# Source order on VectorE and GpSimd ahead of the queries, and one scaling for two input norms

## The chip, the cores and the metric

The kernel runs on one core of one Trainium2 chip. The metric is the device time of one execution in microseconds (us), lower is better. The time of the kernel before is the median of three runs.

## The reference, cut to what matters

A layer of cross attention with a position bias and a mask, then a gated feed-forward layer. Everything is float32: 8 batches of 128 tokens, 512 features, 32 heads of 128, 1376 inner features.

```python
x = x + xattn(layernorm(x), ctx, mask, bias, ...)   # EPS = 1e-5
x = x + ffn(layernorm(x), ...)

def xattn(hidden, kv, ...):
    h = hidden * rsqrt(mean(hidden**2) + EPS) * ln_weight
    q, k, v = h @ w_q.T, kv @ w_k.T, kv @ w_v.T     # 32 heads
    p = softmax(where(mask, q @ k.T + bias, -inf))
    return hidden + (p @ v) @ w_out.T
```

So the attention's input is normalised twice: a layer norm takes away the mean and divides by sqrt(v + EPS), v being the variance; then an RMS norm divides by the root mean square of the result, and multiplies by `ln_weight`. The mean square after the first norm is v / (v + EPS). Both divisions together are one: by sqrt(v (1 + EPS) + EPS²).

## The kernel before

**Stages.** The heads are worked in 8 groups of 4. A prologue loads the context (already transposed), the weights of the first keys and values and the inputs, computes the keys and values of group 0, and normalises and transposes the inputs of the 8 batches. Then come the query projections of all 8 groups, which are stored to DRAM; then attention, group by group, with the keys and values of the next group computed in between; the output projection; the second norm and the feed-forward layer. The diff touches only what is issued ahead of the queries.

**Projections with seven products.** Each projection is a 2x2 block product by Strassen's scheme as Winograd orders it: seven products of half-size blocks in place of eight. GpSimd makes four sums of weight blocks (`sums_a`, lines L194 to L197: s1, s2, a block replaced in place, s4), in a tile `S_k`, `S_v` or `S_q`. Four sums of token blocks (`sums_b`, L202 t1, L203 t2, L204 `b12` replaced in place, L205 t4) are made once for the context (`ctx_sb`) and once for the normed inputs (`hT`); three run on VectorE, L204 on GpSimd.

`seven` then issues the products in the order 2, 1, 6, 7, 4, 5, 3, each for two tiles, and yields after each tile. Products 2, 6, 7 and 4 end with a ScalarE copy out of the PSUM bank (L236, L246). Products 1, 5 and 3 end with a VectorE add (L241 for product 1, L252 for 5 and 3). Products 1, 6, 7 and 4 build up in the same two PSUM banks, so product 6 of a tile can't start before product 1's add has read it, and product 7 not before product 6's copy. Product 6 uses the weight sum s2 and the token sum t2, product 7 the replaced blocks, product 4 the token sum t4.

Of the 28 yields of the prologue (n = 0 to 27), the first 4 are the products 2 and 1 of the keys, then 4 of the values, 10 more of the keys, 10 more of the values. A matmul in float32 shows up as two instructions in the profile, so one product of the keys with its two tiles is eight of them.

**Norms.** For each batch, `norm1` takes the moments (`bn_stats`, `bn_aggr`), the root of the variance (`rstd_of`: a VectorE step, a ScalarE square root, a VectorE reciprocal), subtracts and scales on VectorE into y (L167), squares y on ScalarE with a sum (L172), makes a second root from it, and scales y into `hn` on ScalarE (L176). `norm1_T` transposes `hn` on TensorE (L153), and VectorE multiplies the transposed block by `ln_weight` into `hT` (L181). Before, `norm1` of batch b is called at n = 5 + 2b and `norm1_T` at n = 11 + 2b.

**What sets the order.** Each engine runs its own queue in order. The order within a queue is chosen by the framework's planner: it simulates the program with a cost model and takes, for each engine, the instruction that comes first in the source among those that are ready in the simulation. Source order is thus a priority and not the order. Buffers of a pool (three y slots of tag "s", which the attention's bias additions of L297 use later; four `hn`; two S tiles; three weight tiles) are handed on when their readers are done. Loads are issued on the SP queue (the first weights on ScalarE's).

Of the kernel before, what the change touches and what calls it, by code (L numbers as in the profile page):

```python
# [10 lines left out]
F32 = mybir.dt.float32  # L11
U8 = mybir.dt.uint8
AF = mybir.ActivationFunctionType
ALU = mybir.AluOpType
# [3 lines left out]
P = 128  # L18
BS = 32
EPS = 1e-5  # L20
MASKED = 3.0e38
FLOOR = -1.0e38
TINY = 1.0e-30


@with_exitstack
def xattn_ffn_kernel(
# [19 lines left out]
    nc = tc.nc  # L47
    B, S, D = x.shape
# [13 lines left out]
    ADD, SUB = ALU.add, ALU.subtract  # L62
# [11 lines left out]
    work = pool("work", 2, side="right", reuse_waits="tile")  # L74
    small = pool("small", 4, side="right", reuse_waits="tile")
# [22 lines left out]
    ctx_sb = toks.tile([P, DC + 3, T], F32, tag="ctx", name="ctx_sb")  # L98
# [22 lines left out]
    x_in = [acts.tile([P, 2, D], F32, tag="a", name=f"x_{i}") for i in range(B // 2)]  # L121
    for b in range(B):
        nc.sync.dma_start(x_in[b // 2][:, b % 2, :], x[b])
    q_w = {0: load_q(0)}

    lnw_sb = const.tile([P, DC], F32, name="lnw_sb")
    nc.gpsimd.dma_start(lnw_sb, lnw.rearrange("(c p) -> p c", p=P))
    mask_u8 = work.tile([P, B, S], U8, tag="tt", name="mask_u8")
# [12 lines left out]
    def rstd_of(dst, src, scale):  # L141

        nc.vector.tensor_scalar(dst, src, scale, EPS, ALU.mult, ALU.add)
        nc.scalar.activation(dst, dst, AF.Sqrt)
        nc.vector.reciprocal(dst, dst)

    def moments(mv, b, st, src):
        nc.vector.bn_stats(st, src)
        nc.vector.bn_aggr(mv[:, b, :], st)
# [6 lines left out]
    hT = hpool.tile([P, DC + 3, T], F32, tag="hT", name="hT")  # L156
    mv1 = const.tile([P, B, 2], F32, name="mv1")
    rs1 = const.tile([P, B], F32, name="rs1")

    def norm1(b):  # L160
        st = small.tile([P, nc.vector.BN_STATS_DIM], F32, tag="st", name=f"st_{b}")
        xb = x_in[b // 2][:, b % 2, :]
        moments(mv1, b, st, xb)
        rs = rs1[:, b : b + 1]
        rstd_of(rs, mv1[:, b, 1:2], 1.0)
        y = work.tile([P, D], F32, tag="s", name=f"y_{b}", bufs=3)
        nc.vector.tensor_scalar(  # L167
            y, xb, mv1[:, b, 0:1], rs, ALU.subtract, ALU.mult
        )
        sq = work.tile([P, D], F32, tag="aT", name=f"sq_{b}")  # L170
        ss = small.tile([P, 1], F32, tag="ss", name=f"ss_{b}")
        nc.scalar.activation(sq, y, AF.Square, accum_out=ss)  # L172
        rr = small.tile([P, 1], F32, tag="rr", name=f"rr_{b}")
        rstd_of(rr, ss, 1.0 / D)
        hn = work.tile([P, D], F32, tag="pT", name=f"hn_{b}", bufs=4)
        nc.scalar.activation(hn, y, AF.Copy, scale=rr)  # L176
        return b, hn

    def norm1_T(b, hn):
        tp = transposed(hn, ps_tp.tile([P, DC, P], F32, tag="pt", name="tp"))  # L180
        nc.vector.tensor_tensor(  # L181
            hT[:, :DC, bass.ts(b, S)], tp, lnw_sb.unsqueeze(2).to_broadcast([P, DC, P]), ALU.mult
        )

# [7 lines left out]
    def sums_a(eng, a11, a12, a21, a22, s1, s2, s4):  # L192

        eng.tensor_tensor(s1, a21, a22, ADD)  # L194
        eng.tensor_tensor(s2, s1, a11, SUB)
        eng.tensor_tensor(a21, a11, a21, SUB)
        eng.tensor_tensor(s4, a12, s2, SUB)  # L197
        return {1: a11, 2: a12, 3: s4, 4: a22, 5: s1, 6: s2, 7: a21}

    def sums_b(eng, b11, b12, b21, b22, t1, t2, t4, eng3=None):  # L200

        eng.tensor_tensor(t1, b12, b11, SUB)  # L202
        eng.tensor_tensor(t2, b22, t1, SUB)  # L203
        (eng3 or eng).tensor_tensor(b12, b22, b12, SUB)  # L204
        eng.tensor_tensor(t4, b21, t2, SUB)  # L205
        return {1: b11, 2: b21, 3: b22, 4: t4, 5: t1, 6: t2, 7: b12}

    def combine_rows(name, w):

        a11, a12 = w[:, :HC, :HW], w[:, HC:, :HW]  # L210
        a21, a22 = w[:, :HC, HW:], w[:, HC:, HW:]
        s = spool.tile([P, 3, HC, HW], F32, tag="S", name=f"S_{name}")
        s1, s2, s4 = s[:, 0], s[:, 1], s[:, 2]
        return sums_a(nc.gpsimd, a11, a12, a21, a22, s1, s2, s4)

    def combine_tokens(src):

        b11, b12 = src[:, :HC, :512], src[:, :HC, 512:]
        b21, b22 = src[:, HC:DC, :512], src[:, HC:DC, 512:]
        t1, t2, t4 = (  # L220
            src[:, DC + i, :].rearrange("p (c n) -> p c n", c=HC) for i in range(3)
        )
        return sums_b(nc.vector, b11, b12, b21, b22, t1, t2, t4, nc.gpsimd)

    def seven(name, tiles, product, part, pool, tag="mm"):


        def bank(i):
            return [
                pool.tile([P, 512], F32, tag=tag, name=f"mm_{name}_{i}_{t}") for t in tiles  # L230
            ]

        m = bank(2)
        for t in tiles:
            product(2, t, m[t], True)
            nc.scalar.copy(part(1, 1, t), m[t])  # L236
            yield
        m = bank(1)
        for t in tiles:
            product(1, t, m[t], True)  # L240
            nc.vector.tensor_tensor(part(1, 1, t), part(1, 1, t), m[t], ADD)  # L241
            yield
        for i, r, c in ((6, 1, 2), (7, 2, 2), (4, 2, 1)):
            for t in tiles:
                product(i, t, m[t], False)
                nc.scalar.copy(part(r, c, t), m[t])  # L246
                yield
        m = bank(5)
        for i, r, c in ((5, 2, 2), (3, 1, 2)):
            for t in tiles:  # L250
                product(i, t, m[t], i == 5)
                nc.vector.tensor_tensor(part(r, c, t), part(r, c, t), m[t], ADD)  # L252
                yield

    def project_T(name, w, src, heads):

        for j in range(GH):
            heads.append(acts.tile([P, T], F32, tag="a", name=f"{name}_{j}"))

        def product(i, t, out, first):  # L260
            for c in range(HC):
                nc.tensor.matmul(  # L262
                    out, w[i][:, c, bass.ts(t, P)], src[i][:, c, :],
                    start=(first and c == 0), stop=(c == HC - 1), skip_group_check=True,
                )

        def part(r, c, t):
            return heads[2 * (r - 1) + t][:, bass.ts(c - 1, 512)]

        yield from seven(name, range(2), product, part, ps_mm)  # L270
# [22 lines left out]
    def probabilities(g, b, qT, kT, pb):  # L293
# [22 lines left out]
        ri = small.tile([P, GH], F32, tag="ri", name=f"ri_{n}")  # L316
        nc.vector.tensor_scalar_max(ri, sm, TINY)
        nc.vector.reciprocal(ri, ri)
# [53 lines left out]
    def kv(g, out):  # L372
        wk, wv = kv_w.pop(g)
        kT, v = [], []
        out[g] = kT, v
        keys = project_T(f"k{g}", combine_rows(f"k{g}", wk), ctx_t, kT)
        if g:
            yield from keys
            yield from project_V(f"v{g}", combine_rows(f"v{g}", wv), ctx_t, v, ps_mm)
        else:  # L380

            yield from itertools.islice(keys, 4)
            values = project_V(f"v{g}", combine_rows(f"v{g}", wv), ctx_t, v, ps, "sc")
            yield from itertools.islice(values, 4)
            yield from keys
            yield from values


    queries = [dram.tile([P, GH, T], F32, name=f"queries_{g}") for g in range(NG)]
    ctx_t = combine_tokens(ctx_sb)  # L390
    kvs = {}
    normed = []
    for n, _ in enumerate(kv(0, kvs)):
        if n % 2 == 1 and 5 <= n < 5 + 2 * B:
            normed.append(norm1((n - 5) // 2))
        if n % 2 == 1 and 11 <= n < 11 + 2 * B:
            norm1_T(*normed.pop(0))
    for n in normed:
        norm1_T(*n)
    h_t = combine_tokens(hT)  # L400

    res_scale = const.tile([P, B], F32, name="res_scale")
    res_bias = const.tile([P, B], F32, name="res_bias")
    nc.vector.tensor_scalar_add(res_scale, rs1, 1.0)
    nc.vector.tensor_tensor(res_bias, mv1[:, :, 0], rs1, ALU.mult)
    nc.vector.tensor_scalar_mul(res_bias, res_bias, -1.0)
# [85 lines left out]
    for g in range(NG):  # L492
        kT, v = kvs.pop(g)
# [89 lines left out]
    for i in range(B // 2):  # L583
# [8 lines left out]
        m = by_product(banks)  # L592
        x1.append(acts.tile([P, 2, D], F32, tag="a", name=f"x1_{i}"))
        for k in range(2):
            b = 2 * i + k
# [3 lines left out]
                bias=res_bias[:, b : b + 1], scale=res_scale[:, b : b + 1],  # L599
# [63 lines left out]
    for y in ys:  # L663
        norm2_T(*y)
    t1, t2, t3, t4 = (
        acts.tile([P, HC, 512], F32, tag="a", name=f"T{n}_h2") for n in range(1, 5)
    )
# [7 lines left out]
    for i in range(NP):  # L675
        ws, gate = [], [acts.tile([P, T], F32, tag="a", name=f"gate_{i}_{r}") for r in range(2)]
        for nm, w in zip("gu", gate_up[i]):
            s = fw.tile([P, 3, HC, P], F32, tag="S", name=f"S_{nm}{i}")
# [16 lines left out]
        def part(r, c, t):  # L695
            return (gate[r - 1], act[2 * i + r - 1])[t][:, bass.ts(c - 1, 512)]
# [16 lines left out]
    for b in range(B):  # L713
        r = work.tile([P, D], F32, tag="aT", name=f"r_{b}")
        parts = 1 if b + 1 < B else 2
        for k in range(parts):
            cols = bass.ts(k, D // parts)
            o = ps.tile([P, D // parts], F32, tag="m", name=f"dn_{b}_{k}")
            for n, ic in enumerate([NI - 1, *range(NI - 1)]):
                m = min(P, INTER - ic * P)  # L720
# [50 lines left out]
```

## Time and profile before

| | us |
|---|---|
| median of 3 runs | 1152.23 (1151.07 to 1153.02) |
| the profiled execution, its own time | 1152.01 |
| its span in the profile | 1150.2 |
| TensorE busy (matmul) | 1120.0, 97% of the span |
| VectorE busy | 502.3, 44% |
| ScalarE busy | 318.1, 28% |
| GpSimd busy | 297.9, 26% |
| start of the first query product | 68.9 |

Engines in the profile: PE is TensorE's matmul, PEld its weight load, DVE VectorE, ACT ScalarE, POOL GpSimd, SP the queue of SyncE that issues DMAs. A group's row gives line, engine, operation, out<-in, number, busy time and mean ns. A timeline row gives start and duration in us from the start of the span; the brackets tell how long the engine was idle before it and what released it. A windows row gives a stretch, busy time with the number of instructions for each engine, the granted TensorE clock (1.00 is full), the DMA share, and GB/s.

### The profile page before, as it was taken

What the parts mean: (1) busy time and instruction counts of PE and PEld (TensorE: products, weight loads), DVE (VectorE), ACT (ScalarE), POOL (GpSimd) and SP (SyncE); (2) the same over time, 40 slices, a digit from 0 to 9 for tenths busy, and PEclk for the clock granted to TensorE, in tenths of its full rate; (3) what the DMA queues carried; (4) which work ended last, traced back from release to release, by engine and by line L of the source; (5) the groups of instructions that cost most, each with busy time, mean ns of one, the idle gap of its engine ahead of it and who ended that gap; (6) DMA issues with size and microseconds to landing.
All of it is one profiled execution on the core that took longest, in us unless ns stands there. A gap on an engine that the chain in (4) does not pass through costs nothing.

```text
span 1150.2 us, 12321 instructions
## 1 busy us (share of the span) xinstructions
PE 1120.0 (97%) x4286; PEld 731.4 (64%) x4286; DVE 502.3 (44%) x957; ACT 318.1 (28%) x899; POOL 297.9 (26%) x255
## 2 busy tenths in 40 slices
PE   6999999999999999999999999789999999999998
PEld 3564444445867777686958689678888864444445
DVE  4541111116555555555555557824433242434311
ACT  2521112223444344444344443301000022223000
POOL 5331221116333333333223315620000034220000
PEclk9999999999999999999999999899999999999999
DMA  9114432257555455555554347865232332110000
GB/s 284 41 37 149 175 114 110 110 197 259 175 166 175 151 186 174 168 182 183 179 173 152 129 139 218 275 192 171 78 104 65 109 128 73 36 37 1 18 29 28
DMA packets 117533, 154.38 MB, mean 134 GB/s; under 512 B 12032, under 2 KB 71680, under 8 KB 117472
## 3 DMA queue, kind: packets, MB, share of 16 engines
q1 hardware_dynamic: 114784, 149.93, 40.3%
q10 hardware_dynamic: 2192, 2.10, 0.6%
q0 software_dynamic: 496, 1.58, 0.4%
q8 instruction: 34, 0.56, 0.2%
q14 instruction: 27, 0.22, 0.1%
HBM read 101.14 MB, written 52.43 MB: 134 GB/s over the span
## 4 chain that ended last, share of the span: by engine, by line
PE 91%; DVE 4%; DMA 2%; ACT 1%; issue 1%; POOL 0%; SPq 0%; ACTq 0%; DVEq 0%
PE mm_q L262 17%; PE mm_v L280 16%; PE m L470 16%; PE mm_k L262 16%; PE mm_f L690 9%; PE dn L721 7%; PE sc L302 4%; PE av L358 4%; DMA wk<-in_wkT_dram 1%; DMA wo<-in_woT_dram 1%; PE tp L153 1%; PE up L655 1%; PE gp L655 1%; DVE sg L641 1%; ACT s L312 0%
## 5 line engine op out<-in xcount | busy, mean ns | idle before, releaser
L297 POOL TENSOR_TENSOR s<-pb,mneg 128x512 f32<-128x512 f32 x64 | 81.2, 1269 | 291.1 <-DVE tt L335 217.3
L262 PE MATMUL mm_k<-ctx_sb,wk 128*128 128x512 f32 x256 | 117.8, 604 | 7.2 <-DMA wk<-in_wkT_dram 4.4
L280 PE MATMUL mm_v<-wv,ctx_sb 128*128 128x256 f32 x512 | 115.9, 379 | 0.8 <-DMA wv<-in_wvT_dram 0.8
L262 PE MATMUL mm_q<-hT,wq 128*128 128x512 f32 x256 | 112.5, 592 | 0.0
L312 ACT ACTIVATE s<-s,nmx 128x128 f32<-128x128 f32 x256 | 99.5, 390 | 36.0 <-DVE nmx L309 36.0
L470 PE MATMUL m<-wo,a 128*128 128x256 f32 x400 | 101.5, 392 | 6.6 <-DMA a<-att 6.5
L280 PEld LDWEIGHTS mm_v<-wv,ctx_sb 128*128 128x128 f32 x512 | 95.1, 190 | 14.4 <-DMA wv<-in_wvT_dram 1.6
L363 ACT COPY aT<-av 128x512 f32<-128x512 f32 x64 | 37.5, 586 | 203.3 <-PE av L358 105.4
L262 PE MATMUL mm_k<-ctx_sb,S_k 128*128 128x512 f32 x192 | 88.3, 607 | 4.3 <-DVE k L241 3.9
L470 PEld LDWEIGHTS m<-wo,a 128*128 128x128 f32 x400 | 77.7, 197 | 18.0 <-DMA a<-att 6.8
L262 PEld LDWEIGHTS mm_q<-hT,wq 128*128 128x128 f32 x256 | 48.6, 190 | 60.8 <-issue 60.7
L280 PE MATMUL mm_v<-S_v,ctx_sb 128*128 128x256 f32 x384 | 86.6, 381 | 0.0
L262 PEld LDWEIGHTS mm_k<-ctx_sb,wk 128*128 128x128 f32 x256 | 47.2, 194 | 60.1 <-issue 45.5
L262 PE MATMUL mm_q<-hT,S_q 128*128 128x512 f32 x192 | 85.0, 592 | 0.0
L305 DVE TENSOR_TENSOR s<-sc,s 128x512 f32<-128x512 f32 x64 | 44.2, 690 | 86.8 <-PE sc L302 83.6
L280 PEld LDWEIGHTS mm_v<-S_v,ctx_sb 128*128 128x128 f32 x384 | 71.5, 190 | 11.0 <-DVE v L252 1.8
L302 PEld LDWEIGHTS sc<-k,q 128*128 128x128 f32 x512 | 67.3, 194 | 17.4 <-issue 13.4
L721 PE MATMUL dn<-wd,act 128*128 128x512 f32 (+3 forms) x198 | 75.8, 545 | 0.0
L252 DVE TENSOR_TENSOR q<-q,mm_q 128x512 f32<-128x512 f32 x32 | 22.0, 688 | 114.8 <-PE mm_q L262 114.8
L302 PE MATMUL sc<-k,q 128*128 128x128 f32 x512 | 68.1, 277 | 2.0 <-DMA q<-queries 1.9
L358 PE MATMUL av<-pT,v 128*128 128x128 f32 x512 | 68.1, 277 | 0.0
L262 PEld LDWEIGHTS mm_k<-ctx_sb,S_k 128*128 128x128 f32 x192 | 35.4, 192 | 49.3 <-issue 35.7
(156 smaller groups left out, 1492.1 us busy)
## 6 DMA issues: line engine op xcount, KB each, us to landing
queries<-q SPq DMA_DIRECT2D x32, 512.0 KB, 3.8
q<-queries SPq DMA_DIRECT2D x32, 512.0 KB, 4.4
turned<-tt SPq DMA_DIRECT2D x64, 256.0 KB, 2.1
pT<-turned SPq DMA_DIRECT2D x256, 64.0 KB, 2.4
att<-aT SPq DMA_DIRECT2D x64, 256.0 KB, 2.3
a<-att SPq DMA_DIRECT2D x32, 512.0 KB, 3.5
wq<-in_wqT_dram SPq DMA_DIRECT2D x8, 1024.0 KB, 5.5
wk<-in_wkT_dram SPq DMA_DIRECT2D x7, 1024.0 KB, 6.1
```

What stands on the lines that cost most here:

```text
L262: nc.tensor.matmul(out, w[i][:, c, bass.ts(t, P)], src[i][:, c, :], start=(first and c == 0), stop=(c == HC - 1), skip_group_check=True,)
L280: nc.tensor.matmul(out[:, bass.ts(k, HW)], src[i][:, c, bass.ts(2 * t + k, S)], w[i][:, c, :], start=(first and k == 0 and c == 0), stop=( ...
L297: nc.gpsimd.tensor_tensor(s, pb, mneg[:, b : b + 1, :].to_broadcast([P, GH, S]), ALU.add)
L302: nc.tensor.matmul(sc[:, j, :], qT[:, j, bass.ts(b % 2, S)], kT[j][:, cols], start=True, stop=True)
L305: nc.vector.tensor_tensor(s, sc, s, ALU.add)
L312: nc.scalar.activation(s[:, j, :], s[:, j, :], AF.Exp, bias=nmx[:, j : j + 1], accum_out=sm[:, j : j + 1],)
L358: nc.tensor.matmul(av[:, j, :], v[b // 2][:, b % 2, bass.ts(j, P)], pT[:, :, j, :], start=True, stop=True,)
L363: nc.scalar.copy(aT, av)
L470: nc.tensor.matmul(m[n], sa[n][:, c, :], wo_t[g][n][:, c, :], start=(g == order[0] and c == 0 and k % 2 == 0), stop=(g == order[-1] and c ...
L655: nc.tensor.matmul(o[-1][:m], w[:, c, :m], h2[c // HC, th][:, c % HC, :], start=(c == 0), stop=(c == DC - 1),)
L690: nc.tensor.matmul(out, ws[t][n][:, c, :], h2_t[n][:, c, :], start=(first and c == 0), stop=(c == HC - 1), skip_group_check=True,)
L721: nc.tensor.matmul(o, act[ic][:m, bass.ts(b, S)], wd[:m, ic, cols], start=(n == 0), stop=(n == NI - 1),)
```

## The change

- A wrapper, `InOrder`, calls an engine's operation and then `tc.keep_in_program_order`, which pins the instruction behind the one that was issued just before it on the same engine in the source: an edge of order, without a semaphore. From the loads to the queries all sums, adds and norm steps on VectorE and GpSimd go through it. Afterwards both names point at the plain engines again. TensorE, ScalarE and the DMA queues are not pinned.
- The four context sums are no longer issued together at the start, but one by one: t1 ahead of the keys, t2 and `b12` after the third yield, t4 after the values' product 1. The four sums of `hT` are issued after the last yield, pinned too.
- `norm1` is split in `norm1_moments` and `norm1_scale`. Both norms are one scaling: ScalarE's Identity with scale `rr` and bias `nm` = -mean · rr, straight from x. y, its square and its second root are gone. The reciprocal root of the layer norm, which the residual needs (`rs1`), is made once for all batches after the sums.
- The yields after which moments, scalings and transposes are called are listed by hand.

```diff
+class InOrder:
+    def __init__(self, tc, engine):
+        self.tc, self.engine = tc, engine
+    def __getattr__(self, op):
+        def call(*args, **kw):
+            return self.tc.keep_in_program_order(getattr(self.engine, op)(*args, **kw))
+        return call
...
+    vector, gpsimd = InOrder(tc, nc.vector), InOrder(tc, nc.gpsimd)
...
-    def norm1(b):
+    def norm1_moments(b):
         st = small.tile([P, nc.vector.BN_STATS_DIM], F32, tag="st", name=f"st_{b}")
         xb = x_in[b // 2][:, b % 2, :]
-        moments(mv1, b, st, xb)
-        rs = rs1[:, b : b + 1]
-        rstd_of(rs, mv1[:, b, 1:2], 1.0)
-        y = work.tile([P, D], F32, tag="s", name=f"y_{b}", bufs=3)
-        nc.vector.tensor_scalar(
-            y, xb, mv1[:, b, 0:1], rs, ALU.subtract, ALU.mult
-        )
-        sq = work.tile([P, D], F32, tag="aT", name=f"sq_{b}")
-        ss = small.tile([P, 1], F32, tag="ss", name=f"ss_{b}")
-        nc.scalar.activation(sq, y, AF.Square, accum_out=ss)
+        vector.bn_stats(st, xb)
+        vector.bn_aggr(mv1[:, b, :], st)
         rr = small.tile([P, 1], F32, tag="rr", name=f"rr_{b}")
-        rstd_of(rr, ss, 1.0 / D)
+        vector.tensor_scalar(rr, mv1[:, b, 1:2], 1.0 + EPS, EPS * EPS, ALU.mult, ALU.add)
+        nc.scalar.activation(rr, rr, AF.Sqrt)
+        return b, rr
+
+    def norm1_scale(b, rr):
+        xb = x_in[b // 2][:, b % 2, :]
+        vector.reciprocal(rr, rr)
+        nm = small.tile([P, 1], F32, tag="nm", name=f"nm_{b}")
+        vector.scalar_tensor_tensor(nm, mv1[:, b, 0:1], -1.0, rr, ALU.mult, ALU.mult)
         hn = work.tile([P, D], F32, tag="pT", name=f"hn_{b}", bufs=4)
-        nc.scalar.activation(hn, y, AF.Copy, scale=rr)
+        nc.scalar.activation(hn, xb, AF.Identity, bias=nm, scale=rr)
         return b, hn
...
-    def combine_tokens(src):
+    def token_sums(src):
...
+        sums = [
+            partial(vector.tensor_tensor, t1, b12, b11, SUB),
+            partial(vector.tensor_tensor, t2, b22, t1, SUB),
+            partial(gpsimd.tensor_tensor, b12, b22, b12, SUB),
+            partial(vector.tensor_tensor, t4, b21, t2, SUB),
+        ]
+        return {1: b11, 2: b21, 3: b22, 4: t4, 5: t1, 6: t2, 7: b12}, sums
...
-            yield from itertools.islice(keys, 4)
+            ctx_sums[0]()
+            yield from itertools.islice(keys, 3)
+            ctx_sums[1]()
+            ctx_sums[2]()
+            yield from itertools.islice(keys, 1)
             values = project_V(f"v{g}", combine_rows(f"v{g}", wv), ctx_t, v, ps, "sc")
             yield from itertools.islice(values, 4)
+            ctx_sums[3]()
             yield from keys
             yield from values
...
     for n, _ in enumerate(kv(0, kvs)):
-        if n % 2 == 1 and 5 <= n < 5 + 2 * B:
-            normed.append(norm1((n - 5) // 2))
-        if n % 2 == 1 and 11 <= n < 11 + 2 * B:
+        if n in (3, 6, 8, 9, 10, 12, 14, 16):
+            scales.append(norm1_moments(len(scales) + len(normed) + transposed1))
+        if n in (6, 8, 9, 10, 12, 14, 16, 18):
+            normed.append(norm1_scale(*scales.pop(0)))
+        if n in (10, 11, 12, 14, 16, 18, 20, 22):
             norm1_T(*normed.pop(0))
-    for n in normed:
-        norm1_T(*n)
-    h_t = combine_tokens(hT)
+            transposed1 += 1
+    h_t, h_sums = token_sums(hT)
+    for form in h_sums:
+        form()
+    vector, gpsimd = nc.vector, nc.gpsimd
...
+    rstd_of(rs1, mv1[:, :, 1], 1.0)
     nc.vector.tensor_scalar_add(res_scale, rs1, 1.0)
```

The weight sums (`combine_rows`), the adds of `seven` and the multiplication in `norm1_T` change only from `nc.vector` and `nc.gpsimd` to `vector` and `gpsimd`.

More of the change, by code (lines that the diff above doesn't have):

```diff
@@ L180, in norm1_T @@
         tp = transposed(hn, ps_tp.tile([P, DC, P], F32, tag="pt", name="tp"))
-        nc.vector.tensor_tensor(
+        vector.tensor_tensor(
             hT[:, :DC, bass.ts(b, S)], tp, lnw_sb.unsqueeze(2).to_broadcast([P, DC, P]), ALU.mult
@@ L213, in combine_rows @@
         s1, s2, s4 = s[:, 0], s[:, 1], s[:, 2]
-        return sums_a(nc.gpsimd, a11, a12, a21, a22, s1, s2, s4)
-    def combine_tokens(src):
+        return sums_a(gpsimd, a11, a12, a21, a22, s1, s2, s4)
+    def token_sums(src):
         b11, b12 = src[:, :HC, :512], src[:, :HC, 512:]
@@ L222, in combine_tokens @@
         )
-        return sums_b(nc.vector, b11, b12, b21, b22, t1, t2, t4, nc.gpsimd)
+        sums = [
[5 more added lines that the diff above has]
+        return {1: b11, 2: b21, 3: b22, 4: t4, 5: t1, 6: t2, 7: b12}, sums
     def seven(name, tiles, product, part, pool, tag="mm"):
@@ L240, in seven @@
             product(1, t, m[t], True)
-            nc.vector.tensor_tensor(part(1, 1, t), part(1, 1, t), m[t], ADD)
+            vector.tensor_tensor(part(1, 1, t), part(1, 1, t), m[t], ADD)
             yield
@@ L251, in seven @@
                 product(i, t, m[t], i == 5)
-                nc.vector.tensor_tensor(part(r, c, t), part(r, c, t), m[t], ADD)
+                vector.tensor_tensor(part(r, c, t), part(r, c, t), m[t], ADD)
                 yield
@@ L375, in kv @@
         out[g] = kT, v
-        keys = project_T(f"k{g}", combine_rows(f"k{g}", wk), ctx_t, kT)
+        rows_k = combine_rows(f"k{g}", wk)
+        keys = project_T(f"k{g}", rows_k, ctx_t, kT)
         if g:
@@ L389, in xattn_ffn_kernel @@
     queries = [dram.tile([P, GH, T], F32, name=f"queries_{g}") for g in range(NG)]
-    ctx_t = combine_tokens(ctx_sb)
+    ctx_t, ctx_sums = token_sums(ctx_sb)
     kvs = {}
-    normed = []
+    normed, transposed1 = [], 0
+    scales = []
     for n, _ in enumerate(kv(0, kvs)):
-        if n % 2 == 1 and 5 <= n < 5 + 2 * B:
-            normed.append(norm1((n - 5) // 2))
-        if n % 2 == 1 and 11 <= n < 11 + 2 * B:
-            norm1_T(*normed.pop(0))
-    for n in normed:
-        norm1_T(*n)
-    h_t = combine_tokens(hT)
+        if n in (3, 6, 8, 9, 10, 12, 14, 16):
[3 more added lines that the diff above has]
+        if n in (10, 11, 12, 14, 16, 18, 20, 22):
+            norm1_T(*normed.pop(0))
+            transposed1 += 1
[3 more added lines that the diff above has]
+    vector, gpsimd = nc.vector, nc.gpsimd
     res_scale = const.tile([P, B], F32, name="res_scale")
     res_bias = const.tile([P, B], F32, name="res_bias")
+    rstd_of(rs1, mv1[:, :, 1], 1.0)
     nc.vector.tensor_scalar_add(res_scale, rs1, 1.0)
```

## The prediction

> **What bounds the kernel now.** I read the busy shares first, then the slices, the waits by stage, and the timeline of the first 70 us.
>
> ```profile
> PE 1120.0 (97%) x4286; PEld 731.4 (64%) x4286; DVE 502.3 (44%) x957; ACT 318.1 (28%) x899; POOL 297.9 (26%) x255
> PE   6999999999999999999999999789999999999998
> PEclk9999999999999999999999999899999999999999
> ```
>
> TensorE (PE) is busy for 1120.0 of 1150.2 us and sets the end, so an edit is worth the PE idle time that it removes, no more. The diff touches only what is issued before the queries, so I look at that stretch. The windows table (stretch, then busy time and count per engine, granted clock, DMA share, GB/s):
>
> ```profile
> 0.00:21.88 21.88, 16.61 (x48) 9.85 (x48) 6.68 (x7) 4.81 (x6) 8.31 (x12) 1.00 0.95 316
> 21.88:25.92 4.04, 0.17 (x1) 0.03 (x1) 4.04 (x13) 0.61 (x3) 4.04 (x4) 1.00 0.83 161
> 25.92:31.43 5.51, 5.51 (x8) 1.73 (x8) 5.45 (x18) 3.33 (x12) 4.85 (x4) 0.69 0.46 129
> 31.43:34.18 2.75, 0.00 (x1) 0.03 (x1) 2.75 (x14) 2.75 (x9) 0.00 (x0) 1.00 0.01 3
> 34.18:68.89 34.71, 34.71 (x144) 24.40 (x145) 15.50 (x38) 12.82 (x30) 9.76 (x8) 1.00 0.19 61
> ```
>
> Until 21.88 the DMA is full (0.95). From 34.18 to the first query product at 68.89 PE has no gap. Between lie two holes, 4.04 and 2.75 us, and eight matmuls that take 5.51 us at a clock of 0.69, where the same eight take 3.43 elsewhere (15.00 to 18.43). Who is late is in the timeline (start, duration, engine, line, operation):
>
> ```profile
> 17.73 1.95 DVE L203 TENSOR_TENSOR ctx_sb<-ctx_sb 128x1024 f32<-128x1024 f32 x1
> 18.55 3.33 POOL L204 TENSOR_TENSOR ctx_sb<-ctx_sb 128x1024 f32<-128x1024 f32 x1
> 20.27 2.70 DVE L205 TENSOR_TENSOR ctx_sb<-ctx_sb 128x1024 f32<-128x1024 f32 x1
> 21.84 2.24 POOL L195 TENSOR_TENSOR S_k<-S_k,wk 128x512 f32<-128x512 f32 x1
> 25.11 0.67 DVE L241 TENSOR_TENSOR k<-k,mm_k 128x512 f32<-128x512 f32 x1
> 25.70 2.53 DVE L167 TENSOR_SCALAR y<-x,mv,rs 128x512 f32<-128x512 f32 x2
> 25.92 5.51 PE L262 MATMUL mm_k<-ctx_sb,S_k 128*128 128x512 f32 x8 [3.87 <-DVE k L241]
> 33.47 0.56 ACT L246 COPY k<-mm_k 128x512 f32<-128x512 f32 x1
> 34.18 3.80 PE L262 MATMUL mm_k<-ctx_sb,wk 128*128 128x512 f32 x8 [2.75 <-ACT rr L144]
> ```
>
> The key add L241 has its input from PE at 16.9 us (the first four of eight matmuls from 15.00), yet starts at 25.11: the sums L203 and L205, moments and norm steps stand ahead of it on VectorE (DVE). Product 6 reuses its PSUM bank and waits. The second key add is late in the same way (28.30), behind two y. Then product 7 waits for a ScalarE (ACT) copy of a bank that PE had filled by 29.1 but that starts at 33.47, behind squares, square roots and scalings. GpSimd (POOL) is late too: product 6 also needs L195, done at 24.08, behind L204.
>
> **The Trainium skill.** *TensorE: Matmul & The Clock Gate*, Architectural detail: VectorE and ScalarE run their queues strictly first in, first out. The adds above agree. Same page, What's actually happening: an idle window of about 3.4 us halves the PE clock. Here it followed the 4.04 us hole (0.69 over 5.51 us). *SBUF — State Buffer*, Who interferes with whom: a DVE instruction with two SBUF inputs and a GpSimd one that reads SBUF exclude each other, one instruction at a time. The trace agrees: L202 alone takes 1.22 us, L203 beside POOL 1.95, L205 2.70; L204 3.33 here and 2.35 later.
>
> **The change, part by part.** *Removed:* per batch one y (L167, 747 ns mean), on ACT one square (624 and 187 ns for its sum), one square root (about 0.2) and two or three 0.15 us steps on DVE. Over eight batches this is 5.9 us of DVE and 8 of ACT beside PE's stream; it pays only where PE waits for those queues, and is inside the sum below. *Added:* one 128x1 DVE step for the negated mean, about 0.15 us by the like steps (L143). It reads two SBUF tensors, so by the SBUF page it can wait for a POOL sum (1.26 us, L196). The scaling becomes Identity with scale and bias from memory: *ScalarE: Activation LUTs*, What ACT_TABLE_LOAD costs, prices one more pointer operand at 93 ns, so I estimate 0.72 + 0.09 = 0.81 us a batch; the trace of before has no such instruction at this stage. I bound the extra between 0 and 0.2. One root for all eight rs1 and its two DVE steps replace eight; nothing on PE reads them until far later: cost 0. No DMA is moved or added, SP's queue keeps its order; loads that wait for a weight slot start as much earlier as PE does.
>
> *Moved:* the order on DVE and POOL. I lay the source's order on the measured durations, letting DVE and POOL alternate at the shared port:
> - POOL: key sums from 14.90: s1 to 16.2, s2 to 17.4, a21 to 18.7; s4 lets L203 pass, to 21.2; then the context's b12 (2.3) to 23.4; the four value sums to 29.8.
> - DVE: t1 13.80 to 15.02; key add 16.9 to 17.6; t2 waits for a21, 18.7 to 19.9; second key add to 20.6; moments 0 (0.7); value add from 21.3; moments 1 and scale 0, its negated mean waiting for b12, to 23.5; value add to 24.1; t4 after a value sum, 24.7 to 25.9; then a batch each about 1.3 us: negated means at 27.2, 28.5, 29.9.
> - PE: product 6 needs the first key add (17.6) and s2 (17.4): it starts at **21.88**, with no hole and so no halved clock. Product 7 at 21.88 + 3.44 = 25.32 needs b12 (23.4). Transposes of batch 0 at 27.04 need its scaled input (23.5 + 0.8). Product 4 near 29.6 needs t4 (25.9).
>
> If nothing else is late, product 7 starts at 25.32 instead of 34.18, and the 34.7 us to the queries stay. **Gross gain 8.86 us** (4.04 + 2.08 slow clock + 2.75).
>
> Two things come back. First, ACT: its order is still the planner's, and there a scaling may stand ahead of a copy. If scaling 1 (ready at 27.2, ends at 28.0) precedes the copy of the second product-6 bank, that copy ends at 28.6 and product 7's second half waits from 27.48: 1.2 us; scalings 2 and 3 ahead of the next copy (31.3 against 30.85) cost 0.5. Bounds 0 and 1.7; I take **0.8**, the middle, because I can't see the planner's times. Second, the norm's own sums L202 to L205: before, L202 ran at 66.59, ahead of the last value adds; now all follow them, hence the last value product (query start Q). Product 6 of the queries starts at Q + 6.87 and needs a query add queued behind t4. With free ports: last value add to Q + 0.9, t1 2.1, t2 3.3, t4 behind POOL's b12 (2.3) 6.9, add 7.6, so 0.75 us late. With the next query weights' first two sums also on POOL (their slot comes free at Q) and alternation: t1 2.7, t2 5.2, b12 7.4, t4 8.6, add 9.3: 2.45 late. If DVE passes first, 0.25. I take **1.5**; bounds 0.2 and 2.5.
>
> Net: 8.86 - 0.8 - 1.5 = 6.6 us. The profiled execution took 1152.01 us (span 1150.2), 0.2 below the median of 1152.23; so 1145.4 on its terms, **1145.5** against the median. PE's other idle time (6.5 us on attention results from DMA, among others) follows its own stage and shifts along.
>
> **Rivals.** *Partial:* the hole at product 7 stays, since only DVE and POOL are pinned. For it: its releaser is ACT. Against it: ACT has 3.7 us of work in 3.9 us of PE's pace at most (two copies 1.2, square roots and scalings of at most two batches 2.0, less later). If 2.75 stays whole beside both give-backs' middle, the gain is 8.86 - 2.75 - 1.5 = 4.6: 1147.6; if ACT runs later still, about 1149.
>
> *Slower:* the additions of mask and position bias (L297) float ahead on POOL. They are not pinned, and the normed copies y held their three slots: the wait list has 12.4 us of POOL's L297 ahead of 43.17 ending with ACT's norm. With y gone only the bias tile holds them, and it lands at 29.3 on chip (the issue list: 4 us and more after 24.90). A planner that takes it as landed earlier could queue them before b12. One ahead: b12 ends at 29.3 + 1.3 + 2.3 = 32.9, PE loses another 1.7 us to the clock, and with 1.5 at the queries this is 32.9 - 34.18 + 1.7 + 1.5 = 1.9 worse, 1154: no measurable change. All three ahead: 2.6 more, **1156.6**. It decides from the second on. Against it: POOL's pinned chain is ready without a gap from 14.90, so there is little room to slip in.
>
> *Does nothing:* the planner would have kept this order anyhow. The timeline excludes it: L205 ran before L241, which the source now puts ahead.
>
> **How the numbers follow.** Forecast 0.60; partial 0.20; L297 with one ahead, or other trims that cancel, 0.07; slower 0.13. 0.2% (2.3 us) is about what a measurement of this kernel can tell from no change. Faster 0.80, same 0.07, slower 0.13. The forecast's own bounds are 8.86 - 0.2 = 8.7 and 8.86 - 4.2 = 4.7 us, 1143.5 to 1147.6; with 1 us for later stages falling differently, and the partial rival, the range is 1142.5 to 1150.0.
>
> **What would show it.** Right: product 6 of the keys starts within 0.5 us of 21.9, PEclk stays 1.00 between 26 and 30, the first query product starts between 60 and 62, L241 on k starts near 17, and no y is left. The ACT step is wrong if PE waits for copies L246 longer than 1.7 us; the query step if PE waits for L241 on q longer than 2.5. The whole is wrong if product 7 starts later than 30 us, or if L297 stands before the context's L204 on POOL, or if idle time of more than 2 us appears on PE after 80 us that was not there.

## The result and the profile after

The changed kernel takes **1146.93 us** (median of 6 runs, 1144.04 to 1147.55) against 1151.65 us before (6 runs): ratio 0.9956, 95% interval 0.9943 to 0.9968. It is 4.7 us or 0.4% faster; forecast were 6.6 us. A second set on another occasion gave 1146.59 against 1151.92, again 0.9956 (0.9939 to 0.9972). The profiled execution took 1146.99 us, its span is 1145.2.

The page's busy shares and clock slices, after:

```profile
PE 1114.6 (97%) x4286; PEld 728.7 (64%) x4286; DVE 500.2 (44%) x943; ACT 312.2 (27%) x876; POOL 297.9 (26%) x255
PEclk9999999999999999999999999899999999999999
```

VectorE lost 2 us and ScalarE 6 us of busy time in all, which would explain nothing by itself: PE still sets the end. The windows of the prologue, in the same stretches as before but for the last (the first busy time after the stretch's length is PE's):

```profile
0.00:21.88 21.88, 15.79 (x49) 9.84 (x50) 6.79 (x10) 5.01 (x7) 9.10 (x13) 1.00 0.95 312
21.88:25.92 4.04, 4.04 (x11) 1.77 (x10) 3.95 (x6) 1.49 (x3) 3.96 (x3) 1.00 0.87 172
25.92:31.43 5.51, 3.32 (x11) 1.51 (x10) 5.20 (x17) 2.95 (x8) 5.41 (x5) 1.00 0.50 138
31.43:34.18 2.75, 2.75 (x13) 1.58 (x12) 2.01 (x7) 1.37 (x5) 2.00 (x2) 1.00 0.00 0
34.18:62.00 27.82, 27.82 (x121) 20.77 (x120) 12.54 (x31) 8.06 (x16) 5.00 (x4) 1.00 0.24 77
```

The two old holes (4.04 and 2.75 us) are full of PE's work and the clock is 1.00 throughout, but in the third stretch PE is idle for 2.19 of 5.51 us. Who causes that is in the timeline (line L34 is the wrapper of all pinned instructions):

```profile
16.93 0.69 DVE L34 TENSOR_TENSOR k<-k,mm_k 128x512 f32<-128x512 f32 x1 [1.45 <-PE mm_k L285]
21.83 3.60 PE L285 MATMUL mm_k<-ctx_sb,S_k 128*128 128x512 f32 x8
22.37 1.36 DVE L34 SCALAR_TENSOR_TENSOR nm<-mv,rr 128x1 f32<-128x1 f32 x1
25.26 1.89 PE L285 MATMUL mm_k<-ctx_sb,wk 128*128 128x512 f32 x4
27.12 1.26 POOL L34 TENSOR_TENSOR wv<-wv 128x512 f32<-128x512 f32 x1
27.14 1.26 DVE L34 SCALAR_TENSOR_TENSOR nm<-mv,rr 128x1 f32<-128x1 f32 x1
28.44 0.81 ACT L193 ACTIVATE hn<-x,nm,rr 128x512 f32<-128x512 f32 x1 [1.16 <-DVE nm L34]
29.16 0.56 ACT L269 COPY k<-mm_k 128x512 f32<-128x512 f32 x1
29.77 1.98 PE L285 MATMUL mm_k<-ctx_sb,wk 128*128 128x512 f32 x4 [2.19 <-ACT k L269]
```

The key add starts as soon as PE delivers (at 16.93, where it was 25.11 before); product 6 follows at 21.83 without a hole, product 7 at 25.26, **8.92 us earlier** than before. But the copy that product 7's second half needs, ready at 25.4, starts at 29.16: behind the scaling of batch 1. That one waits for a negated mean of one element per partition, which takes 1.26 us beside a GpSimd sum.

At the start of the queries (62.23 us) a second hole appears:

```profile
63.04 6.20 DVE L34 TENSOR_TENSOR hT<-hT 128x1024 f32<-128x1024 f32 x3
65.91 2.25 POOL L213 TENSOR_TENSOR wq<-wq 128x512 f32<-128x512 f32 x1
69.17 1.27 DVE L264 TENSOR_TENSOR q<-q,mm_q 128x512 f32<-128x512 f32 x2
69.98 3.67 PE L285 MATMUL mm_q<-hT,S_q 128*128 128x512 f32 x8 [0.72 <-DVE q L264]
```

Three token sums that take 1.22 us each alone fill 6.20 us, taking turns with GpSimd; the query add waits behind them.

Where the time is, from the start of the same matmuls in both traces:

| | before | after |
|---|---|---|
| product 7 of the keys starts | 34.18 | 25.26 (-8.92) |
| first query product | 68.89 | 62.23 (-6.66) |
| from there to the queries' product 6 | 6.87 | 7.75 |
| first score product of the attention | 261.16 | 255.46 (-5.70) |
| output projection, its first product to the first gate product | 233.72 | 234.50 |
| from there to the end | 215.99 | 216.02 |

### The profile page after: what moved, and what is told of

Read it like the earlier page. It is cut to its first block, busy times and chain, and to the rows that moved or that the text cites. A ratio compares the mean times of both kernels' runs of the same rounds, so it can differ in the third digit from the quotient of the medians.

```text
span 1145.2 us, 12293 instructions
## 1 busy us (share of the span) xinstructions
PE 1114.6 (97%) x4286; PEld 728.7 (64%) x4286; DVE 500.2 (44%) x943; ACT 312.2 (27%) x876; POOL 297.9 (26%) x255
## 4 chain that ended last, share of the span: by engine, by line
PE 92%; DVE 4%; DMA 2%; ACT 1%; issue 1%; POOL 0%; ACTq 0%; SPq 0%; DVEq 0%
PE mm_v L303 17%; PE m L505 16%; PE mm_q L285 16%; PE mm_k L285 16%; PE mm_f L725 9%; PE dn L756 7%; PE sc L325 5%; PE av L381 5%; DMA wv<-in_wvT_dram 1%; DMA wo<-in_woT_dram 1%; PE tp L168 1%; PE up L690 1%; PE gp L690 1%; DVE sg L676 1%; DVE hT L34 0%
## 5 line engine op out<-in xcount | busy, mean ns | idle before, releaser
L320 POOL TENSOR_TENSOR s<-pb,mneg 128x512 f32<-128x512 f32 x64 | 81.1, 1269 | 276.1 <-DVE tt L358 217.2
L285 PEld LDWEIGHTS mm_q<-hT,S_q 128*128 128x128 f32 x192 | 36.4, 190 | 47.0 <-issue 47.0
```

Of the source, the lines that this page charges most:

```text
L285: nc.tensor.matmul(out, w[i][:, c, bass.ts(t, P)], src[i][:, c, :], start=(first and c == 0), stop=(c == HC - 1), skip_group_check=True,)
L320: nc.gpsimd.tensor_tensor(s, pb, mneg[:, b : b + 1, :].to_broadcast([P, GH, S]), ALU.add)
```

## The experiments

Each was timed in five rounds beside the kernel before, in three sets, whose medians of before are 1151.65, 1151.92 and 1151.73. "Changed kernel" is the one with the whole change.

**Set 1: which part carries it.** *Without the pinning:*

```diff
-    vector, gpsimd = InOrder(tc, nc.vector), InOrder(tc, nc.gpsimd)
+    vector, gpsimd = nc.vector, nc.gpsimd
```

> Everything of the change but the pinning: both names stay the plain engines, so the planner orders VectorE and GpSimd. Theory (the order carries the gain): VectorE takes t1, moments, t2 and t4 ahead of the key adds again, the first key add starts after 24 us instead of 16.9, product 6 of the keys starts at 24.5 to 26, TensorE's clock is halved for one window, and only part of the second hole goes: 1148.5 to 1151. Rival (the shorter norms carry it, since they free VectorE and ScalarE): product 6 starts before 23 us and the time is within 1 us of the changed kernel's 1146.9.

Measured: **1157.21 us**, ratio 1.005 (1.0037 to 1.0063), slower than before. Both theories missed the size: the first query product starts at 73.22, 4.33 us later than before. Its timeline:

```profile
19.92 0.20 ACT L184 ACTIVATE rr<-rr 128x1 f32<-128x1 f32 x1 [5.93 <-DVE rr L183]
20.03 1.05 ACT L259 COPY v<-mm_v 128x512 f32<-128x512 f32 x2
20.65 5.41 PE L303 MATMUL mm_v<-wv,ctx_sb 128*128 128x256 f32 x16 [1.98 <-ACT v L259]
24.38 0.66 DVE L264 TENSOR_TENSOR k<-k,mm_k 128x512 f32<-128x512 f32 x1
34.27 3.75 PE L285 MATMUL mm_k<-ctx_sb,wk 128*128 128x512 f32 x4 [4.78 <-ACT k L269]
69.69 3.69 PE L303 MATMUL mm_v<-S_v,ctx_sb 128*128 128x256 f32 x16 [2.10 <-DVE v L275]
```

The key add is late again (24.38) and product 6 starts at 25.90, as the theory said. Three more waits came that it did not name: the value copies stand on ScalarE behind batch 0's square root, which waits for VectorE's moments (1.98 us; from 21.3 to 24.7 the clock is half); the key copies stand behind roots and scalings of many batches (4.78, so product 7 starts no earlier than before); and the last value adds stand behind the sums of `hT` (2.10). So the order on VectorE decides when ScalarE's queue moves, though nothing on ScalarE is pinned in the changed kernel.

*Pinning and order of the sums with the two old norms* (y, square and second root called at yields of their own):

```diff
+        y = work.tile([P, D], F32, tag="s", name=f"y_{b}", bufs=3)
+        vector.tensor_scalar(
+            y, x_in[b // 2][:, b % 2, :], mv1[:, b, 0:1], rs, ALU.subtract, ALU.mult
+        )
...
+        nc.scalar.activation(sq, y, AF.Square, accum_out=ss)
...
+        if n in (7, 9, 10, 11, 13, 15, 17, 19):
+            normed.append(norm1_rms(*halves.pop(0)))
```

> The pinning and the order of the sums, but the two norms as they were (y, square, second root), their steps called at about the same yields. Theory (order): product 6 starts at 21.9 with a full clock; the longer norms on ScalarE and the pinned VectorE steps that wait for ScalarE's roots make the hole at product 7 longer than the 2.2 us of the changed kernel, 3 to 5 us: 1147 to 1150. Rival (norms): without the shorter norms nearly nothing is gained, 1150.5 or more.

Measured: 1148.20 us, ratio 0.9975 (0.9965 to 0.9985), in the range of the order theory. The hole of 3 to 5 us at product 7 did not come in one piece: product 6 starts at 21.55 and product 7 at 25.53; then PE waits 2.0 us in two parts for key copies and 1.2 us for a transpose's input, and part of the work behind these runs at half clock. The first query product comes at 64.82, 2.59 us later than with joined norms. The yields of the second root and its scaling were chosen for this run, so a better list for the old norms may exist.

*Pinned on one engine only* (`nc.gpsimd`, then `nc.vector`, in place of its wrapper):

> Pinned on VectorE only; GpSimd's order is the planner's (the value sum s1 goes ahead of the key sum s2, the rest stays). Theory (VectorE's order is what counts): s2 comes one sum (1.3 us) later, at about 19.3 us, still ahead of 21.8, so the time is that of the changed kernel within 0.7 us: 1146.2 to 1147.6. Rival (both orders are needed): product 6 or 7 waits for GpSimd and the time is 1148.5 or more.

> Pinned on GpSimd only. Theory (VectorE's order counts): as without any pinning, key add after 24 us, product 6 at 24.5 to 26, 1148.5 to 1151. Rival (GpSimd's late sum s2 was the hole): product 6 starts before 23 us, 1146 to 1148.

Measured: VectorE alone 1146.15, ratio 0.9952 (0.9939 to 0.9966), the changed kernel's; GpSimd alone **1156.31**, ratio 1.0045 (1.003 to 1.006), about as slow as no pinning at all. So the pinned order on VectorE is the gain. The list of sums and its pinning were not separated further: the new places without pinning gain nothing (1157.21), and pinning with the sums in their old places was not run. The order on GpSimd costs about as much as it gives: without it, `b12` of the context comes later and product 7 waits for it:

```profile
26.61 1.98 PE L285 MATMUL mm_k<-ctx_sb,wk 128*128 128x512 f32 x4 [1.48 <-POOL ctx_sb L409]
```

but the negated mean of batch 0 gets its turn between two sums at once (0.18 us at 21.87), that of batch 1 ends at 26.57 in place of 28.40, and the wait for the key copy is gone (first query product at 61.22).

**Set 2: what the two new holes are.** *The changed kernel again:*

> The changed kernel once more, beside the three below, on the same chip: 1146.9 within 1 us; the hole ahead of product 7's second half and the one ahead of the queries' product 6 are there again, 2.2 and 0.7 us.

Measured: 1146.59 us; waits of 2.1 us for the key copy and 0.7 for the query add.

*Copies ahead of scalings:*

```diff
+    def after_copies(b):
+        return InOrder(tc, nc.scalar) if b else nc.scalar
...
-        nc.scalar.activation(hn, xb, AF.Identity, bias=nm, scale=rr)
+        after_copies(b).activation(hn, xb, AF.Identity, bias=nm, scale=rr)
...
-        if n in (6, 8, 9, 10, 12, 14, 16, 18):
+        if n in (6, 10, 11, 12, 13, 14, 16, 18):
```

(the root in `norm1_moments` likewise; moments at 3, 6, 9, 10, 11, 12, 14, 16; transposes at 10, 12, 13, 14, 16, 18, 20, 22)

> The square roots and scalings of batches 1 to 7 are pinned on ScalarE behind the copy that was issued before them, and are called one to two yields later, so that the copies of products 6 and 7 go first. Theory (the 2.2 us hole at product 7 is a copy queued behind a scaling): product 7's second half starts at 27.4 to 27.7, no wait for ScalarE over 0.5 us, and the time falls by 1.7 to 2.3 us against the changed kernel: 1144.7 to 1145.3. Rival (ScalarE isn't the limit, VectorE's negated means are): the hole moves to the transposes or to product 4, and less than 0.7 us is won.

Measured: 1144.12 us, ratio 0.9931 (0.9918 to 0.9945). No wait of PE for ScalarE is left in the prologue, and the first query product starts at 59.58, 2.65 us earlier than in the changed kernel. The negated means still take up to 1.35 us and delay scalings, but PE no longer waits for a copy behind one. The edit moves calls as well as the order, so it shows that the hole goes when no late scaling stands ahead of the copy, not which of the two moves did it.

*The negated mean with one tensor input:*

```diff
-        vector.scalar_tensor_tensor(nm, mv1[:, b, 0:1], -1.0, rr, ALU.mult, ALU.mult)
+        vector.tensor_scalar(nm, mv1[:, b, 0:1], rr, -1.0, ALU.mult, ALU.mult)
```

> The negated mean as a tensor_scalar step with the reciprocal root as its scalar operand, so it reads one SBUF tensor and a scalar in place of two tensors. Theory (the 1.26 and 1.36 us of two such steps are waits for the port that GpSimd's sums hold): they fall to about 0.15, scaling 1 starts at about 27.3 in place of 28.44, and the hole at product 7's second half shrinks from 2.2 to about 1.1: 1145.8. Rival (the scalar operand waits for the port as well, or the wait is another): they stay over 1 us, time unchanged.

Measured: **1142.41 us**, ratio 0.9918 (0.9905 to 0.9930), more than expected. Its timeline:

```profile
21.18 2.35 POOL L34 TENSOR_TENSOR ctx_sb<-ctx_sb 128x1024 f32<-128x1024 f32 x1
22.19 0.21 DVE L34 TENSOR_SCALAR nm<-mv,rr 128x1 f32<-128x1 f32 x1
25.73 0.21 DVE L34 TENSOR_SCALAR nm<-mv,rr 128x1 f32<-128x1 f32 x1
25.98 0.81 ACT L193 ACTIVATE hn<-x,nm,rr 128x512 f32<-128x512 f32 x1
26.70 0.57 ACT L269 COPY k<-mm_k 128x512 f32<-128x512 f32 x1
27.32 1.98 PE L285 MATMUL mm_k<-ctx_sb,wk 128*128 128x512 f32 x4
```

All eight steps take 0.21 us, the first in the middle of GpSimd's 2.35 us sum. I had counted only the second wait. The first goes too, so everything behind it on VectorE, t4 included, moves up; scaling 1 starts at 25.98 in place of 28.44, the copy ends in time, and the whole hole is gone, with scalings still ahead of copies. First query product: 59.78. That is 2.45 us of the prologue. So the hole needed both, a scaling ahead of the copy and a negated mean that held up the scaling. The median fell by 4.2 us against the changed kernel of the same set; the other 1.7 us were not in the prologue, and lie within the spread of that kernel's runs there (1143.91 to 1149.37).

*The sums of the normed inputs earlier:*

```diff
+    h_t, h_sums = token_sums(hT)
     for n, _ in enumerate(kv(0, kvs)):
...
+        for form in {22: h_sums[:1], 24: h_sums[1:3], 26: h_sums[3:]}.get(n, ()):
+            form()
-    h_t, h_sums = token_sums(hT)
-    for form in h_sums:
-        form()
```

> The four sums of the normed inputs are issued at yields 22, 24, 24 and 26 in place of after the last yield, the pinning kept. Theory (the query add waits behind t4): the 0.9 us between the start of the queries and their product 6 goes, 7.75 becomes 6.87 us: 1146.0. Rival (the adds of the value products now wait behind the sums): TensorE waits at the last value products and the time is the same or up to 1 us longer.

Measured: 1144.90 us, ratio 0.9939 (0.9927 to 0.9951). The queries' product 6 starts 6.87 us after the first query product and no longer waits; no value product waits either. In its profiled execution the clock was halved for 3.4 us at 30.4, after the 2.1 us hole at product 7, so its attention starts at 255.96, no earlier than the changed kernel's.

**Set 3.** *Both edits together:*

> The changed kernel with the negated mean reading one tensor and the sums of the normed inputs at yields 22 to 26. If the two holes (2.2 us at product 7, 0.9 at the queries' product 6) are separate, both are gone: queries start at about 59.8, their product 6 6.87 us later, and the time is 0.9 below that of the one-input kernel: 1141.5. If the earlier sums delay the last value adds, it is 1142.4 or more.

Measured: **1141.59 us** (1140.89 to 1144.08), ratio 0.9920 (0.9906 to 0.9934): faster than the kernel before and than the changed one. From the kernel with the one-input mean alone (0.9918) the ratio can't be told apart; what the earlier sums add is seen in the trace only. PE's waits of the prologue (what waits, for whom: us, times, longest):

```profile
PE mm_k L285 <- DMA wk<-in_wkT_dram: 4.6, 1, 4.6
PE mm_v L303 <- DMA wv<-in_wvT_dram: 1.2, 1, 1.2
```

Only the first loads are left. The first query product starts at 59.67, the queries' product 6 again 6.87 us later, attention at 251.94: 9.22 us earlier than before. So all of the gross gain of the prediction (8.86) can be had.

*Joined norms in the kernel before, nothing else* (`norm1` with `rr`, `nm` and the Identity as one function, called where it was, and the one root for all `rs1`):

```diff
+        nc.vector.scalar_tensor_tensor(nm, mv1[:, b, 0:1], -1.0, rr, ALU.mult, ALU.mult)
...
-        nc.scalar.activation(hn, y, AF.Copy, scale=rr)
+        nc.scalar.activation(hn, xb, AF.Identity, bias=nm, scale=rr)
```

> The kernel before with its two norms joined, and nothing else: the sums, the yields of the calls (5 + 2b, 11 + 2b) and the planner's freedom stay. Theory (without the order the shorter norms buy nothing): VectorE still has t1, moments, t2, t4 ahead of the key adds, product 6 starts at 24.5 to 26 and the clock is halved; the planner puts all square roots and four scalings ahead of the first key copy, so product 7 starts at 31.5 to 34.5: 1150 to 1152.5. Rival (the shorter norms gain by themselves, and the unpinned kernel was slow only because its calls come earlier): product 7 starts before 30 and the time is 1149 or less.

Measured: **1155.42 us**, ratio 1.0031 (1.0020 to 1.0041), slower than before and beyond what I expected. The wait is the one I named, and longer:

```profile
33.98 0.20 ACT L166 ACTIVATE rr<-rr 128x1 f32<-128x1 f32 x1 [2.89 <-DVE rr L165]
34.65 0.21 ACT L144 ACTIVATE rs<-rs 128x8 f32<-128x8 f32 x1 [0.47 <-DVE rs L143]
34.77 1.05 ACT L241 COPY k<-mm_k 128x512 f32<-128x512 f32 x2
35.48 4.94 PE L257 MATMUL mm_k<-ctx_sb,wk 128*128 128x512 f32 x7 [4.51 <-ACT k L241]
```

The roots of all eight batches, and even the one for `rs1`, stand ahead of the first key copy; on chip the last of them wait for the last batch's moments. That there is less to do per batch, and that the planner therefore takes them first, is my reading; its simulated times can't be seen. Product 7 starts 1.3 us later than before and runs at half clock at first, so the first query product comes at 71.77, 2.88 us later. That is most of the 3.7 us in the medians.

## Why the prediction was right

**The bound and the gross gain: right.** Forecast: product 6 at 21.88, product 7 at 25.32, 8.86 us gross. Measured: 21.83, 25.26, 8.92. The cause, VectorE's order, is shown by pinning it alone (1146.15), by leaving it free (1156.31, 1157.21), and by pinning with the old norms (1148.20). The scaling with two pointers took 0.81 us, as estimated. The net gain is another matter: 6.6 us were forecast, 4.7 measured, and the terms that were taken off were all mis-sized.

**The first give-back was mis-sized.** "I take 0.8, the middle" of 0 to 1.7; measured 2.26 (8.92 at product 7, 6.66 at the first query product), beyond the bound. The place and the mechanism were those named, a scaling ahead of the second product-6 copy. The term that failed is the port: the working lets batch 1's negated mean in when the second value sum ends, at 27.2. That sum did end there (27.17), but the record of the next starts at 27.12 and that of the mean's step at 27.14: the step lost the turn, and waited this sum out too, to 28.40. Scaling 1 ended at 29.25 and the copy at 29.72, where the working has 28.0 and 28.6. The second part, 0.5 us at the next copy, did not occur. By the prediction's own test, a wait for copies over 1.7 us, this step is wrong; and the first query product came at 62.23, just behind the 60 to 62 that it gave.

**The second was mis-sized the other way.** Forecast 1.5, measured 0.88 (7.75 against 6.87), inside the bounds. GpSimd took all four of the next query weights' sums ahead of `b12`, so `b12` held up neither t4 nor the query add; what delayed t4 was taking turns with those four.

**The rest was taken at zero.** The output projection took 0.78 us more in the profiled execution (234.50 against 233.72), but 231.70 in the other profile of the same kernel: 2.8 of the 3.1 us between the spans of these two. So that this 0.78 comes from the change isn't shown. The other stages after the queries' product 6 differ by about 0.1 us at most. The sum is 8.92 - 2.26 - 0.88 - 0.78 = 5.0 us of span, 4.7 in the medians. One sign of "the whole is wrong" did appear: idle time of more than 2 us after 80 us. In the output projection PE is idle for 16.38 us against 13.12 before (and busy for 2.48 us less). In the other profile of the changed kernel it is 13.48, so this idle time comes and goes between executions of one kernel; as a sign it was badly chosen.

**The rivals.** The partial one came closer than the forecast: it has a gain of 4.6 us, the forecast 6.6, measured are 4.7. Much of what it describes happened, too: a hole at product 7 stayed, 2.19 us where it was 2.75, at the second half and with ScalarE as its releaser. The argument against it weighed only ScalarE's own work, and not that a scaling could wait for VectorE while a copy stood behind it. The measured gain lies at the edge of the forecast's own bounds (4.7 to 8.7 us). That it isn't outside them is partly luck: 0.62 us too much was taken off at the queries, and 0.78 us in the output projection were not counted, so these two nearly cancel. The additions L297 (L320 now) did not float ahead: they start at 29.7, after the value sums. That the joined norms help by themselves I had not made a rival; alone they cost 3.7 us in the medians. With the order they seem to add 1.3 to 1.6 (1148.20 against 1146.93 and 1146.59, from different sets; the intervals of the ratios still touch).

## What to carry to other kernels

An engine that is 44% busy can hold back the one that sets the end through the order of its queue alone: look at what stands ahead of the late instruction, and pin the one engine whose order decides. A lighter step under a planner that orders by simulated times isn't a gain by itself, since it changes what is taken first; test it alone. And where a tiny step stands between two heavy engines, try another operand form: its duration alone doesn't show what it will wait for.

## What I had not expected of the hardware

- A step of one element per partition waits as long as a large one: `nm` with two SBUF tensors took 1.36 us beside `b12`, 0.16 undisturbed. The Trainium skill (*SBUF — State Buffer*, Who interferes with whom) states the rule for two inputs, and the trace agrees. With the second operand as a scalar pointer the step took 0.21 us beside the same sum, so here that operand didn't count as a second input. One input is no warrant, though: the step for all eight `rs1`, 128x8 with one tensor input, took 1.17 us beside GpSimd's additions in the kernel without pinning and 0.15 with GpSimd idle in the one with joined norms only. Why it waits there wasn't tested.
- The hole of 2.1 us at product 7 was followed by a halved clock in one profile (at 30.4 us in the kernel with early sums, 2.12 us) and not in two others (the changed kernel's, 2.19 and 2.06 us). Without pinning, a hole of 1.98 us was followed by one and a hole of 2.10 was not; with only GpSimd pinned, 1.91 and 2.10 were and 1.93 was not. So a hole need not be as long as the idle window of about 3.4 us that the prediction cites, and its length alone doesn't decide; here the measurements count. Worked out from the clocks of the windows, the halving lasted about 3.4 us in the kernel before (0.69 over 5.51 us), as in the ones with early sums and without pinning.
- The output projection took between 231.70 and 236.23 us in the profiles, with a mean clock of 0.96 to 0.98, which at half clock makes 10 to 20 us in all (an estimate). Why it was 1.7 us shorter with the one-input mean than in the changed kernel's first profile (232.77 against 234.50) isn't settled; the changed kernel's other profile had 231.70.
